# Masked self-attention with a residual: range checks and loads moved behind the first queries, tails last in the last product, eight buffers and later additions for inactive tokens

## The chip, the cores and the metric

The kernel runs on one core of one Trainium2 chip. The metric is the device time of one execution in microseconds (us); lower is better. A core has TensorE (PE; its weight loads are listed as PEld), VectorE (DVE), ScalarE (ACT), GpSimd (POOL) and SyncE (SP). Each engine works through its own queue of instructions in order. SP issues the plain DMAs, POOL the indirect ones that gather and scatter rows by an index.

## The reference

Sixteen batches of x (512 features x 1024 tokens), a mask of zeros and ones by token, and two 512 x 512 weights. Eight heads of 64 features; queries, keys and values are the same projection.

```python
xt = transpose(x, (0, 2, 1))
q = xt @ Wq.T
qh = q.reshape(B, T, NH, dk).transpose(0, 2, 1, 3)
scores = scale * einsum('bhqd,bhkd->bhqk', qh, qh)
logits = (scores * cmask + (1.0 - cmask) * NEG) * rmask
attn = softmax(logits, axis=-1)
ctx = einsum('bhqk,bhkd->bhqd', attn, qh)
out = ctx.transpose(0, 2, 1, 3).reshape(B, T, D) @ Wo.T
return x + transpose(out, (0, 2, 1))
```

About half of the tokens are masked. An active token attends to the active tokens alone. For a masked token all logits are zero, so its attention is the plain mean over all 1024 tokens and its output is the same for all masked tokens of a batch.

## The kernel before

**Compaction.** For each batch the kernel gathers the active tokens into slots 0 to 543 (`C` = 544: four blocks of 128 and a tail of 32, `CT`) and computes attention on these. Inactive tokens sit in further slots, gathered in blocks j = 5 to 8 (the last of 96 rows); they get one row per batch added, the projected mean (`ub`), and are scattered to the output. A flag at the end says whether the inputs were in the ranges on which this rests (`ok`); only if not, a general path runs.

**Work of one batch.** `gather` fetches the slots' rows (`xa`, tail `xt`, L313). `xt` transposes them on TensorE (L398) and `xsplit` splits them into two float16 parts `xh` and `xl` (L358 on ScalarE, L359 on VectorE). `query(n, e, g)` multiplies by the split weights `wqh`, `wql` (L421; feature block e, half g of the columns), ScalarE evicts (L424), VectorE masks the upper columns (L427). `qsplit` splits a query block into float16 parts `hl` (L435 to L437) and SP spreads them over partitions into `xx` by four DMAs (L442 to L445). `value` transposes q (L467), ScalarE copies it to `v` (L469) and squares are summed for each token (L458, L459). `shift`, made of `top` (L505 to L511) and `bottom` (L518 to L532), turns the largest of these sums into a shift `nm` for the exponential. `scores` multiplies `xx` with itself (L580; the tail rows L555) and ScalarE takes the exponential with row sums (L584, L559). `attend` multiplies by `v` (L598, L601). `recip_sums` and `recip_rows` invert the row sums (L620 to L628), transpose them (L634), and send them through DRAM to a broadcast tile `rb` (L639, L642); `norm` multiplies and splits the context (L665 to L671). `project` multiplies with the split `wo` (L681), adds x (L686) and scatters the block (L765). The tails of two or three batches form a group, which is projected in one product, `project_tail`.

**Means.** The mean over all tokens comes from the untransposed x: SP loads it (`load_half` L337, in halves of 256 KB for batches 0 and 1; `load_all` L348, 512 KB a piece, for the others) and ScalarE sums it (`sum_half`, L343).

**Range checks.** `range_x` takes the largest absolute value of each of the four blocks of `xh` (L366, L368); `range_w` takes that of `wqh` and of `woh` in one instruction each (L373); `ranges` compares all of them at the end (L378 to L386).

**Inactive tokens.** `late` gathers a block into the tile `xi`, of which there are four buffers; `rest` adds `ub` on VectorE (L752) and scatters. The first loads of x for batches 0 and 1 use the same tag `xi`.

**What sets the order.** The framework's scheduler orders each engine's instructions from the order of the program, from priorities (`high_priority`) and from dependences; `behind(ins)` lets the instructions inside it be issued after `ins`, and `once(instruction, ins)` adds a dependence that the instruction waits for on the chip. The first queries of batch 0 are written out as the list `first`. From `self.paced = True` on, `run` walks over 18 steps in each batch (`S`: four pairs of heads times four token blocks, and two tail steps): it issues the scores of this step, then a share of the list `m`, in which the rest of this batch and the preparation of the next one stand with their costs, and the transfers that are due. Gathers and scatters are posted to two lines, `urgent` and `spare`, and at each step one of them is issued (`issue`); it waits for `self.beat`, the last score or query product of TensorE at that point. `self.st[0]["top"]` is the instruction that completes the first shift `nm` (L523). The weights `wo` are loaded by `load("o", c)` (L155) and split by `split` (L162 on ScalarE, L163 on VectorE).

**The end.** `last` makes the last batch's output product: the contributions of three pairs of heads first, then `norm` of the fourth pair, then the remaining products. The product of the tails is cut into three pieces that stand between those of the four blocks.

## Time and profile before

| | |
|---|---|
| Time, median of 3 runs (lowest to highest) | 1118.86 us (1118.13 to 1123.56) |
| The profiled execution: its time, its span | 1119.63 us, 1117.8 us |
| PE busy | 1071.0 us (96%) |
| DVE busy | 731.6 us (65%) |
| ACT busy | 676.8 us (61%) |
| POOL busy | 288.6 us (26%) |
| Moved by DMA | 181.34 MB, mean 162 GB/s |

The profile is of one execution; its span runs from the first to the last instruction. A line of the timeline gives start, duration, engine, line of the kernel, operation, out<-in, shape, count and in brackets the engine's idle time before it with what ended it. A line of the waits reads: who waited, for whom, total us, times, longest. A line of windows gives the stretch, its length, each engine's busy time with the number of instructions, the granted TensorE clock, the busy share of the DMA engines and GB/s.

### The profile page before, as it was taken

To read this page: it belongs to the slowest core of one execution; us is meant where nothing else is said; L and a number is where in the kernel's file an instruction comes from. 1 tells how busy PE (TensorE), PEld (TensorE's weight loads), DVE (VectorE), ACT (ScalarE), POOL (GpSimd) and SP (SyncE) were. 2 spreads that over 40 slices of the span, in tenths; PEclk is the share of its full clock that TensorE was granted. 3 is DMA by queue.
4 is the path that set the end of the run, shared out by engine and by line. 5 is a ranking of instruction groups with operands and counts; after the bars stand their busy time and mean duration, and the time that the engine had idled before them with its cause. 6 is when DMAs were issued, how large, how long until landed. Compare 5 with 4: busy or idle time off the path is not lost.

```text
span 1117.8 us, 23184 instructions
## 1 busy us (share of the span) xinstructions
PE 1071.0 (96%) x8386; PEld 697.7 (62%) x8386; DVE 731.6 (65%) x2369; ACT 676.8 (61%) x1716; POOL 288.6 (26%) x303
## 2 busy tenths in 40 slices
PE   7899999999999999999999999999999999998987
PEld 6576666666666666566666666666666666665543
DVE  6787466765665767667665766857576685655543
ACT  5876666666566666567565665666566666645540
POOL 3101031323202222222222232222222223214542
PEclk9999999999999999999999999999999999999999
DMA  7745455646546464565655566465656654546652
GB/s 235 212 121 155 128 164 150 190 127 185 144 128 177 125 209 142 163 179 159 192 145 173 158 185 182 130 193 146 198 157 176 185 146 146 147 115 194 187 168 72
DMA packets 78121, 181.34 MB, mean 162 GB/s; under 512 B 15008, under 2 KB 16800, under 8 KB 78000
## 3 DMA queue, kind: packets, MB, share of 16 engines
q1 hardware_dynamic: 56816, 111.62, 36.4%
q0 software_dynamic: 21184, 68.18, 19.2%
q8 instruction: 68, 1.11, 0.4%
q14 instruction: 53, 0.43, 0.1%
HBM read 92.34 MB, written 33.91 MB: 113 GB/s over the span
## 4 chain that ended last, share of the span: by engine, by line
PE 63%; DVE 14%; DMA 10%; issue 7%; ACT 3%; POOL 2%; SPq 1%; DVEq 0%; POOLq 0%; ACTq 0%
PE pav L598 17%; PE pss L580 16%; PE pm L681 13%; PE pm L421 8%; DMA xi<-x_in,idx 3%; DMA rb<-rd 2%; PE pm L398 2%; PE pav L601 2%; DMA rd<-rr 2%; ACT p L584 2%; POOL y_out L765 2%; PE pm L467 1%; DVE c L665 1%; PE pm L634 1%; DVE tmp L458 1%
## 5 line engine op out<-in xcount | busy, mean ns | idle before, releaser
L584 ACT ACTIVATE p<-pss,nm 128x544 f32<-128x544 f32 x512 | 363.8, 715 | 219.9 <-PE pss L580 209.6
L580 PE MATMUL pss<-xx 128*128 128x272 f16 x2048 | 303.1, 280 | 5.4 <-DMA xx<-hl 2.6
L598 PE MATMUL pav<-p,v 128*64 128x272 f32 x2048 | 278.9, 402 | 0.9 <-ACT c L605 0.9
L580 PEld LDWEIGHTS <-xx 128*128 128x128 f16 x2048 | 192.4, 99 | 85.2 <-issue 40.2
L598 PEld LDWEIGHTS pav<-p,v 128*64 128x64 f32 x2048 | 131.0, 136 | 98.2 <-issue 38.5
L765 POOL DMA_INDIRECT y_out<-xa,idx x68 | 70.9, 1043 | 304.8 <-PE pss L580 163.6
L421 PE MATMUL pm<-xh,wqh 128*128 128x274 f16 (+1 forms) x512 | 143.7, 281 | 0.1
L421 PE MATMUL pm<-xl,wqh 128*128 128x274 f16 (+1 forms) x512 | 143.2, 280 | 0.2 <-DVE xl L359 0.2
L421 PE MATMUL pm<-xh,wql 128*128 128x274 f16 (+1 forms) x512 | 143.2, 280 | 0.0
L313 POOL DMA_INDIRECT xa<-x_in,idx x68 | 69.3, 1020 | 181.7 <-PE pss L580 89.8
L421 PEld LDWEIGHTS <-wqh 128*128 128x128 f16 x1024 | 99.7, 99 | 23.1 <-issue 4.7
L584 ACT ACTIVATION_READ_ACCUMULATOR p<-pss,nm 128x1 f32 x512 | 102.9, 201 | 0.0
L686 DVE SCALAR_TENSOR_TENSOR xa<-pm,xa 128x512 f32<-128x512 f32 x60 | 41.4, 689 | 87.1 <-PE pm L681 87.0
L313 POOL DMA_INDIRECT xi<-x_in,idx x60 | 59.7, 995 | 145.7 <-PE pss L580 49.0
L424 ACT ACTIVATE q<-pm 128x272 f32<-128x272 f32 (+1 forms) x128 | 51.2, 400 | 69.0 <-PE pm L421 68.7
L681 PE MATMUL pm<-woh,ch 128*128 128x512 f16 x240 | 91.1, 380 | 1.0 <-DVE xa L686 1.0
L681 PE MATMUL pm<-woh,cl 128*128 128x512 f16 x240 | 91.0, 379 | 0.0
L681 PE MATMUL pm<-wol,ch 128*128 128x512 f16 x240 | 90.9, 379 | 0.0
L765 POOL DMA_INDIRECT y_out<-xi,idx x60 | 60.3, 1004 | 89.6 <-PE pss L580 70.6
L665 DVE TENSOR_TENSOR c<-c,rb 128x544 f32<-128x544 f32 x64 | 46.3, 724 | 54.7 <-DMA rb<-rd 48.4
L681 PEld LDWEIGHTS <-ch 128*128 128x128 f16 x480 | 46.3, 98 | 41.8 <-issue 1.2
L752 DVE TENSOR_TENSOR xi<-xi,ub 128x512 f32<-128x512 f32 (+1 forms) x60 | 40.1, 687 | 40.6 <-DMA xi<-x_in,idx 27.7
(191 smaller groups left out, 1584.7 us busy)
## 6 DMA issues: line engine op xcount, KB each, us to landing
xx<-hl SPq DMA_DIRECT2D x256, 136.0 KB
xm<-x_nat_in SPq DMA_DIRECT2D x56, 512.0 KB
rb<-rd SPq DMA_DIRECT2D x128, 136.0 KB
pt<-c SPq DMA_DIRECT2D x64, 136.0 KB
pt<-p SPq DMA_DIRECT2D x64, 136.0 KB
ub<-ud SPq DMA_DIRECT2D x16, 256.0 KB
xi<-x_nat_in SPq DMA_DIRECT2D x8, 256.0 KB
xa<-x_in,idx POOLq DMA_INDIRECT x68, 4.3
```

Source lines behind the costliest of these rows:

```text
L313: dma = self.nc.gpsimd.indirect_dma_start(out=tile[:n], out_offset=None, in_=self.x, in_offset=bass.IndirectOffsetOnAxis(ap=idx, axis=0))
L398: self.pe = nc.tensor.transpose(pt[:, c, :], x[:n, c * P:(c + 1) * P], self.ident[:n, :n]).ins
L421: self.beat = nc.tensor.matmul(pq, lhsT=w[:, c, e * P:(e + 1) * P], rhs=xx[:, c, cols], start=(k == 0), stop=(k == 3 * DC - 1)).ins
L424: nc.scalar.activation(s["q"][:, e, cols], pq, AF.Copy, scale=1.0 / (SX * SW))
L580: self.beat = nc.tensor.matmul(pt[:, g, :CH], lhsT=xx[:, 2 * k, i * P:(i + 1) * P], rhs=xx[:, 2 * k + a, g * CH:(g + 1) * CH], start=(a == ...
L584: self.exp = [nc.scalar.activation(t.rearrange("p (g c) -> p g c", g=2), pt[:, :, :CH], AF.Exp, bias=s["nm"][p // HG][:, p % HG:p % HG + 1 ...
L598: nc.tensor.matmul(s["pav"][k * DK:(k + 1) * DK, g, :CH], lhsT=s["v"][p][:, i, k * DK:(k + 1) * DK], rhs=ps[k][:, cols], start=(i == 1), s ...
L665: nc.vector.tensor_tensor(c, c, s["rb"][p], ALU.mult)
L681: nc.tensor.matmul(po[:cols.stop - cols.start], lhsT=a[:, e, cols], rhs=w[:, e, :], start=(e == 0 and k == 0), stop=(e == DC - 1 and k == 2))
L686: self.nc.vector.scalar_tensor_tensor(x, po, 1.0 / (SX * SW), x, ALU.mult, ALU.add)
L752: self.nc.vector.tensor_tensor(x[:n], x[:n], s["ub"][:n], ALU.add)
L765: dma = self.nc.gpsimd.indirect_dma_start(out=self.out, out_offset=bass.IndirectOffsetOnAxis(ap=idx, axis=0), in_=x, in_offset=None)
```

## The change

It does six things.

1. The range checks of batch 0 and of `wq` are placed behind the first shift (`apart`), and `range_w` is done in four pieces, one for each block of 128 rows; `big` and `okr` get a column for each piece.
2. Of the eight halves of batch 1's x, the first four are loaded where all eight were; the other four are posted at the first paced step and wait for the first shift. Their sums are placed at earlier steps (`k // 3` for `k // 2`).
3. The loads of `wo` and batch 2's loads of x wait for the first shift, too.
4. In `last` the product of the tails is made in one piece behind the four blocks.
5. The tag `xi` has eight buffers instead of four, and the additions of `rest` wait for `self.beat`.
6. The memory in SBUF for descriptors of POOL's DMAs is 4096 bytes a partition (`dynamic_dma_scratch_size`) instead of the default 16384.

```diff
-        self.big = fixed("big", [P, self.B + 2])
+        self.big = fixed("big", [P, self.B + 2 * DC])
...
     def load_half(self, b, k, after=None):
         c, h = k // 2, k % 2
-        t = self.sb([P, T // 2], F32, *((("xm", 2), ("ub", 3), ("xi", 4), ("xi", 4))[k // 2 if b < 2 else 0]))
+        t = self.sb([P, T // 2], F32, *((("xm", 2), ("ub", 3), ("xi", 8), ("xi", 8))[k // 2 if b < 2 else 0]))
...
-    def load_all(self, b, c):
+    def load_all(self, b, c, after=None):
         t = self.sb([P, T], F32, "xm", 2)
-        self.nc.sync.dma_start(out=t, in_=self.x_nat[b, c * P:(c + 1) * P, :])
+        self.once(self.nc.sync.dma_start(out=t, in_=self.x_nat[b, c * P:(c + 1) * P, :]), after)
...
-    def range_w(self, name):
-        wh = self.w[name][0]
-        k = self.B + "qo".index(name)
-        self.nc.vector.tensor_reduce(self.big[:, k:k + 1], wh, AX.XY, ALU.max, apply_absolute_value=True)
+    def range_w(self, name, c):
+        k = self.B + DC * "qo".index(name) + c
+        self.nc.vector.tensor_reduce(self.big[:, k:k + 1], self.w[name][0][:, c, :], AX.X, ALU.max, apply_absolute_value=True)
...
-    def late(self, b, j, tag="xi", bufs=4):
+    def late(self, b, j, tag="xi", bufs=8):
...
         def add():
             x, idx = s["xi"][j]
             n = idx.shape[0]
-            self.nc.vector.tensor_tensor(x[:n], x[:n], s["ub"][:n], ALU.add)
+            self.once(self.nc.vector.tensor_tensor(x[:n], x[:n], s["ub"][:n], ALU.add), self.beat)
...
         self.norm(b, 3)
-        tails = slice(0, len(self.group[b]) * CT)
-        self.product(*s["ct"], tails, pos[4], range(1))
         for i in range(4):
-            if i == 2:
-                self.product(*s["ct"], tails, pos[4], range(1, 3))
             self.project(b, i, pos[i], range(3, DC))
-        self.project_tail(b, pos[4], range(3, DC))
+        self.project_tail(b, pos[4])
...
-        first += [(0, lambda k=k: self.load_half(1, k, self.last_xt)) for k in range(2 * DC)]
+        first += [(0, lambda k=k: self.load_half(1, k, self.last_xt)) for k in range(DC)]
...
         with self.behind(self.st[0]["top"]):
             for _, f in query(0, 1, 1)[1:] + query(0, 2, 1)[1:]:
                 f()
+        first_top = self.st[0]["top"]
+        def apart(f, *a):
+            def run():
+                with self.behind(first_top):
+                    f(*a)
+            return run
...
-        begin += [(0, L(self.load, "o", c)) for c in range(DC)]
-        begin += [(0, L(self.range_x, 0, c)) for c in range(DC)] + [(0, L(self.range_w, "q"))]
+        begin += [(0, L(self.load, "o", c, None, first_top)) for c in range(DC)]
+        begin += [(0, apart(self.range_x, 0, c)) for c in range(DC)] + [(0, apart(self.range_w, "q", c)) for c in range(DC)]
...
-                places = [("xi", 4), ("xa", 13)]
+                places = [("xi", 8), ("xa", 13)]
...
             if b == 1:
-                m.append((0, L(self.range_w, "o")))
+                m += [(0, L(self.range_w, "o", c)) for c in range(DC)]
...
-                    free.setdefault(at, []).append(L(self.load_all, b + 2, c))
+                    free.setdefault(at, []).append(L(self.load_all, b + 2, c, None if b else first_top))
...
             if b == 0:
                 for k in range(3, 2 * DC):
-                    free.setdefault(k // 2, []).append(L(self.sum_half, 1, k))
+                    if k >= DC:
+                        free.setdefault(0, []).append(lambda k=k: self.load_half(1, k, first_top))
+                    free.setdefault(k // 3, []).append(L(self.sum_half, 1, k))
...
-    nc = bacc.Bacc("TRN2", target_bir_lowering=False, num_devices=1)
+    nc = bacc.Bacc("TRN2", target_bir_lowering=False, num_devices=1, dynamic_dma_scratch_size=4096)
```

More of the change, by code (lines that the diff above doesn't have):

```diff
@@ L368, in range_x @@
             nc.vector.tensor_reduce(self.big[:, b:b + 1], s["top4"], AX.X, ALU.max)
-    def range_w(self, name):
-        wh = self.w[name][0]
-        k = self.B + "qo".index(name)
-        self.nc.vector.tensor_reduce(self.big[:, k:k + 1], wh, AX.XY, ALU.max, apply_absolute_value=True)
+    def range_w(self, name, c):
+        k = self.B + DC * "qo".index(name) + c
+        self.nc.vector.tensor_reduce(self.big[:, k:k + 1], self.w[name][0][:, c, :], AX.X, ALU.max, apply_absolute_value=True)
     def ranges(self):
         nc, B = self.nc, self.B
-        ok = self.sb([P, B + 2], F16, "okr")
+        ok = self.sb([P, B + 2 * DC], F16, "okr")
         nc.vector.tensor_scalar(ok[:, :B], self.big[:, :B], XMAX, None, ALU.is_le)
         nc.vector.tensor_scalar(ok[:, B:], self.big[:, B:], WMAX, None, ALU.is_le)
-        pe = self.pm([P, B + 2])
+        pe = self.pm([P, B + 2 * DC])
         nc.tensor.matmul(pe, lhsT=self.on16, rhs=ok, start=True, stop=True)
```

## The prediction

> **What bounds the kernel now.** I read the page's busy row first, then who waited for whom, then the timeline where the longest waits lie.

> ```profile
> span 1117.8 us, 23184 instructions
> PE 1071.0 (96%) x8386; PEld 697.7 (62%) x8386; DVE 731.6 (65%) x2369; ACT 676.8 (61%) x1716; POOL 288.6 (26%) x303
> ...
> PE pm L634 <- DVE rcol L628: 6.5, 6, 2.3
> PE pm L467 <- DVE q L427: 6.4, 7, 2.6
> ...
> PE pss L580 <- DMA xx<-hl: 2.6, 2, 2.2
> ...
> DVE xi L752 <- DMA xi<-x_in,idx: 27.7, 21, 3.6
> ```

> TensorE is busy for 96% of the span, so all that can be won is its 46.8 us of idle time (1117.8 − 1071.0). The wait rows give total, times and longest: TensorE waits for VectorE at the row sums (L634) and the query transposes (L467), once for the first split queries (L580). VectorE in turn stands 27.7 us in front of the inactive tokens' additions (L752), whose gather has not landed. By windows of about 65 us the middle is 96 to 99% busy; the idle time lies in 0–55 us and after 1010 us.

> The start, from the timeline and from windows of 4 us (length, busy times, granted clock, DMA share, GB/s):

> ```profile
> 29.70 2.28 DVE L373 TENSOR_REDUCE big<-wqh 128x1 f32<-128x2048 f16 x1
> 33.18 0.62 PE L580 MATMUL pss<-xx 128*128 128x272 f16 x4 [2.25 <-DMA xx<-hl]
> 36.00 0.71 ACT L584 ACTIVATE p<-pss,nm 128x544 f32<-128x544 f32 x1 [3.83 <-DVE nm L520]
> 24.00:28.00 4.00, 2.73 (x20) 1.76 (x18) 4.00 (x9) 2.55 (x6) 1.68 (x2) 1.00 1.01 358
> 28.00:32.00 4.00, 2.93 (x24) 2.21 (x23) 3.89 (x8) 3.60 (x11) 1.24 (x2) 1.00 0.96 238
> 32.00:36.00 4.00, 1.95 (x15) 1.34 (x16) 1.07 (x6) 0.17 (x3) 0.64 (x1) 1.00 0.99 357
> ```

> VectorE (third busy time) is full until 32 us, partly with range checks nobody needs yet, and the DMA engines are full (share about 1) with eight halves of x; the first exponential starts at 36.00.

> Late, and at the end:

> ```profile
> 1017.27 0.69 DVE L752 TENSOR_TENSOR xi<-xi,ub 128x512 f32<-128x512 f32 x1 [2.96 <-DMA xi<-x_in,idx]
> 1020.37 0.33 PE L467 MATMUL pm<-ident,q 128*128 128x128 f32 x1 [2.55 <-DVE q L427]
> 1019.26:1022.67 3.41, 1.52 (x10) 1.00 0.83 228
> 1022.67:1026.08 3.41, 2.89 (x13) 0.50 0.91 267
> 1106.20 0.96 POOL L765 DMA_INDIRECT y_out<-xa,idx  x1 [12.43 <-DVE xa L686]
> 1111.71 0.96 POOL L765 DMA_INDIRECT y_out<-xa,idx  x1 [0.30 <-issue]
> ```

> An addition blocks VectorE for 2.96 us, the mask L427 behind it is late, TensorE stands 2.55 us, and the next 3.41 us are granted half the clock. The kernel ends with five scatters on POOL, 1106.20 to 1111.71.

> **The change, part by part.** The sum is made against the profiled execution, 1119.63 us (span 1117.8), which is 0.77 us above the median of three, 1118.86.

> *Start.* Taken from VectorE ahead of the first scores: L366 at 24.53 (0.63 us up to the next start), two at 26.83 (1.26), L368 and L373 at 29.64–31.90 (2.26); the one at 22.36 stood before an instruction that waited for TensorE anyway and counts nothing. The row maxima L507 then come not at 32.45 but about 29.6; L509, L511, L518, L520 took 1.3 us (34.66 to 35.96) and now run among the query products, so the shifts nm are there at about 31.2. The other half is the xx transfer. Its split L436 is 0.63 us earlier, and 1 MB of x is no longer ahead of it: 1.05 MB at the 358 GB/s of that window is 2.9 us. The first scores could start at 33.18 − 3.5 = 29.7, before the query products end (30.93), so TensorE goes on at 31.2 with the two small products in between. First exponential about 31.7 instead of 36.00: 4.3 us.

> Behind it ScalarE is full (4.00 of 4 us at 36–44 in the same table). The four wo casts there (0.65 + 0.63 + 0.63 + 0.65, L162 from 42.96) move behind the next xm sum, into 56–68 us where ScalarE was busy 3.38, 1.74 and 2.14 of 4: up to 2.2 us more. Against that VectorE gets the range work at about 33–40: 4 x 0.71, and wq in four pieces. A 512-element piece is not in the trace: between 2.28/4 = 0.57 and the 0.71 of the 545-element L366; I take 0.68, nearer in shape, 2.7 in all and 5.6 with L368. Its cover is VectorE's 5.5 us of idle time at 32–44 (1.07, 3.10 and 2.32 busy of 4), of which the shift leaves about half, and four wol splits (0.69 each) that leave this stretch; without cover the second query's split and its scores are 2 us late. The waits added to loads stand in SP's queue: behind two halves of x, which wait for the shifts (first_top), come the spreads of queries 1 and 2; their hl is itself made after first_top, so they lose 2 x 0.5 us of issue and 0.5 MB of bandwidth (1.5 us). The wo loads and batch 2's xm are now behind query 3's spread, some 15 us later than 31.06; readers are the casts at about 56. Taken: −4.5, ends −2 and −6.5.

> *Additions and eight buffers, 55–1010 us.* A new buffer spares POOL's gather its wait for an old scatter (4.7 us in 3 waits) and the tie to a score product (beat) puts L752 later in VectorE's order, some after L427 instead of before it. TensorE waits just behind a waiting addition at 450 (1.5 us), and with 0.2 to 0.4 us at 247, 508, 715 and 906: about 3 us to win. The price: 60 of 64 additions wait for TensorE too, and behind them now stand L620, L626–L628 (for L634) about twice as often, 0.69 us each. No row shows that wait, so bounds: −3 if VectorE is always late anyway, +5 if seven of them come through. Taken −1, near the gain, because an addition behind beat starts when TensorE has just issued scores and has 1 to 2 us of other work.

> *1010–1026.* The gathers at 1013.77 and 1015.68 waited 1.86 and 0.88 us for scatters to free the buffer; with eight they don't. Without the 2.96 us L427 runs at about 1017.0, before TensorE needs it at 1017.8: 2.55 us. The half-clock window did 1.45 us less than its 2.89 busy. [...] I take −4.0; the wait at L634 (1.30) stays, as one more addition stands before L628.

> *1058–1084.* Additions that wait 3.65 and 2.05 us move behind L628 and L686: TensorE's 0.64 and most of 1.01 go, and the rb transfer that VectorE awaits at 1077.88 is about 1.9 us earlier. But two additions (1.3 us) now lie between it and L628 at 1082.38. Net −0.6, ends −2.5 and +1.5.

> *Tail.* Without the first tail piece (0.77 us, 1103.60 to 1104.37) in front of it, block 0 and its scatter are 0.77 earlier, at 1105.43; the other four follow at POOL's step of 1.27: last at 1110.5 for 1111.71. The tails' twelve products (12 x 0.216) end at 1108.9, its addition at 1109.7, in time. −1.2.

> *At nothing.* wo's range in pieces: 0.4 us of VectorE time in a stretch where it has 14 us of slack (50.52 of 65). [...]

> Sum: 4.5 + 1 + 4 + 0.6 + 1.2 = 11.3. 1119.6 − 11.3 = 1108.3, and 1107.6 beside the median.

> **The rivals.** (1) Only start and tail pay, the new waits eating the rest: −5.7, 1113.2. For it: few of the 27.7 us reach TensorE. Against: the chain 1017 to 1020 is plain. (2) The gain at the start is handed back, as ScalarE's sums or VectorE stand for loads that now come later, and the middle gives nothing: −1.2 to −3, about 1117. For it: VectorE and ScalarE are both full at 36–53. Against: the casts that leave. (3) The other side: the additions' new wait becomes the bound. About 30 of them stand right before the row sums; each that comes through is 0.69 us at L634. All 30 are +20.7 − 11.3: 1128. It turns to a loss from 17 on. For it: L634 and L467 are already TensorE's longest waits; against: in 49 of 64 cases L634 did not wait for VectorE. (4) The order does not change as said: excluded for the start, as the order of instructions shows L373 behind the second query's split and the loads behind the spreads.

> **How the numbers follow.** A measurement tells 0.5%, 5.6 us, from no change: faster is below 1113.3. Likeliest case 0.64 (1101 to 1112; by the ends of its terms a little more); rival 1 0.20, two thirds of it just below 1113.3; rival 2 0.08; rival 3 0.08. Faster 0.64 + 0.14, same 0.06 + 0.08, slower 0.08. The range from 1101 to 1117 leaves out some 0.06 below, part of rival 2 and rival 3.

> **What would show it.** Right: the first L584 at 31–33 us; no L580 wait on xx over 1 us before 40; L752 waits on xi under 12 us in total; no half-clock window between 1000 and 1060; last scatter 1.0 to 1.4 us nearer to the first. Wrong: TensorE waits at L634 well over 12.7 us in total (6.5 + 4.9 + 1.3 before), ScalarE waiting for wo, xi gathers spaced wider than 1.3 us.

## The result and the profile after

The changed kernel takes 1102.14 us (median of 4 runs, 1100.26 to 1102.9), the kernel before 1118.49 us beside it (1116.53 to 1123.56). The ratio is 0.9832, 95% interval 0.9808 to 0.9855: 16.4 us less by the medians. The forecast of 1107.6 had the direction, but 11.3 of the 16.4 us; with the ratio on 1118.86 the time is 1100.1, just under the range of 1101 to 1117. The profiled execution has a span of 1100.9 us and a time of 1102.9.

The page's busy row and the waits of the changed kernel (who waited, for whom, total us, times, longest):

```profile
span 1100.9 us, 23215 instructions
PE 1066.3 (97%) x8386; PEld 695.1 (63%) x8386; DVE 735.7 (67%) x2375; ACT 675.8 (61%) x1716; POOL 295.2 (27%) x303
...
PE pss L555 <- DMA xx<-hl: 2.7, 1, 2.7
PE pm L634 <- DVE rcol L628: 2.4, 4, 0.8
...
PE pm L467 <- DVE q L427: 0.7, 2, 0.4
...
DVE xi L752 <- PE pss L580: 17.2, 20, 1.9
DVE xi L752 <- DMA ub<-ud: 11.7, 4, 3.5
```

TensorE's work is nearly the same (1066.3 for 1071.0); its idle time fell from 46.8 to 34.6 us. The waits for the row sums (L628) fell from 6.5 to 2.4 us and for the query mask (L427) from 6.4 to 0.7. VectorE's 27.7 us in front of the additions for a gather are gone. In their place stand 17.2 us for TensorE's scores, which is the tie itself, and they cost TensorE nothing that shows.

**Where the time went.** Both kernels take the same 512 exponentials L584 in the same order of batches, so the two traces can be cut at the 1st, 33rd, 193rd, 225th, 449th, 481st and last. The windows between those, of before and then of the changed kernel (stretch, length, each engine's busy time, granted clock, DMA share, GB/s):

```profile
36.00:97.00 61.00, 57.83 (x484) 39.79 (x482) 46.80 (x165) 46.86 (x123) 6.60 (x6) 1.00 0.59 160
97.00:433.00 336.00, 328.26 (x2574) 214.60 (x2572) 222.11 (x726) 209.21 (x528) 72.95 (x71) 1.00 0.54 155
433.00:502.00 69.00, 66.45 (x529) 43.09 (x528) 47.30 (x163) 42.01 (x106) 17.66 (x18) 1.00 0.56 160
502.00:963.60 461.60, 455.55 (x3583) 298.89 (x3582) 310.35 (x994) 290.74 (x738) 125.12 (x124) 1.00 0.58 167
963.60:1036.30 72.70, 68.48 (x512) 43.93 (x510) 44.91 (x138) 38.22 (x99) 21.74 (x22) 0.98 0.52 145
1036.30:1091.30 55.00, 50.46 (x355) 28.04 (x355) 27.10 (x82) 28.49 (x75) 26.68 (x27) 0.97 0.58 176
```

```profile
33.20:95.00 61.80, 58.64 (x487) 39.97 (x486) 50.80 (x175) 47.00 (x123) 7.15 (x7) 0.97 0.67 195
95.00:428.70 333.70, 328.18 (x2574) 214.71 (x2572) 222.09 (x725) 208.67 (x529) 72.81 (x71) 1.00 0.54 157
428.70:495.00 66.30, 65.30 (x524) 42.34 (x523) 47.58 (x163) 41.48 (x105) 18.08 (x18) 1.00 0.58 167
495.00:957.10 462.10, 455.93 (x3586) 299.22 (x3585) 312.25 (x995) 290.81 (x737) 128.82 (x124) 1.00 0.57 167
957.10:1025.50 68.40, 67.28 (x513) 43.16 (x512) 45.66 (x140) 38.27 (x99) 22.96 (x22) 1.00 0.53 154
1025.50:1074.80 49.30, 48.76 (x355) 27.12 (x354) 27.54 (x78) 28.35 (x75) 28.34 (x27) 1.00 0.61 192
```

Up to the first exponential −2.8; then +0.8, −2.3, about −2.2 (the cut at 502 is half a microsecond late, which the next row takes back), 0, −4.3, −5.7; behind the last one 26.5 became 26.1, −0.4. The sum is −16.9, the difference of the spans. The two late rows carry 10 of it. They have the granted clock of 0.98 and 0.97 in before (a window of 3.41 us at half clock in each) and 1.00 after.

The start of the changed kernel, from the timeline, and two windows of it:

```profile
33.22 0.71 ACT L584 ACTIVATE p<-pss,nm 128x544 f32<-128x544 f32 x1
39.31 0.28 PE L555 MATMUL pss<-xx 128*32 128x272 f16 x1 [2.65 <-DMA xx<-hl]
37.18:40.60 3.42, 1.29 (x11) 1.00 (x12) 2.77 (x6) 2.18 (x6) 0.00 (x0) 1.00 0.96 254
40.60:44.01 3.41, 3.41 (x26) 1.51 (x25) 1.89 (x5) 1.26 (x3) 0.00 (x0) 0.50 0.65 200
```

The first scores no longer wait for xx; the second query's transfer of xx is now the late one, TensorE stands 2.65 us for it, and a window at half clock follows. Late and at the end, in the timeline:

```profile
1012.50 0.68 DVE L752 TENSOR_TENSOR xi<-xi,ub 128x512 f32<-128x512 f32 x1
1016.89 0.32 DVE L427 TENSOR_TENSOR q<-q,hr 128x160 f32<-128x160 f32 x1
1068.36 0.33 PE L634 MATMUL pm<-ident,rcol 128*128 128x128 f32 x1 [0.54 <-DVE rcol L628]
1089.56 0.96 POOL L765 DMA_INDIRECT y_out<-xa,idx  x1 [12.34 <-DVE xa L686]
1094.62 0.90 POOL L765 DMA_INDIRECT y_out<-xg,tails  x1 [0.30 <-issue]
```

The addition at 1012.50 has no bracket: its rows are there. The transpose L634 stands 0.54 us; in before it stood 2.30, in a window in which TensorE was 1.50 us busy, and the next window was at half clock:

```profile
1082.61 0.33 PE L634 MATMUL pm<-ident,rcol 128*128 128x128 f32 x1 [2.30 <-DVE rcol L628]
1080.70:1084.11 3.41, 1.50 (x12) 0.84 (x12) 1.98 (x9) 1.13 (x4) 0.93 (x2) 1.00 0.77 226
1084.11:1087.52 3.41, 3.41 (x17) 2.23 (x14) 0.00 (x0) 1.46 (x5) 0.41 (x1) 0.50 0.53 154
```

### The profile page after: what moved, and what is told of

Same layout as the page of the kernel before. It is cut to its first block, busy times and chain, and to the rows that moved or that the text cites. A ratio compares the mean times of both kernels' runs of the same rounds, so it can differ in the third digit from the quotient of the medians.

```text
span 1100.9 us, 23215 instructions
## 1 busy us (share of the span) xinstructions
PE 1066.3 (97%) x8386; PEld 695.1 (63%) x8386; DVE 735.7 (67%) x2375; ACT 675.8 (61%) x1716; POOL 295.2 (27%) x303
## 4 chain that ended last, share of the span: by engine, by line
PE 72%; DVE 14%; DMA 6%; issue 4%; ACT 3%; SPq 1%; POOL 0%; DVEq 0%; POOLq 0%; ACTq 0%
PE pav L598 20%; PE pss L580 17%; PE pm L681 15%; PE pm L421 8%; PE pm L398 3%; PE pav L601 2%; DMA rb<-rd 2%; PE pm L467 2%; DVE c L665 2%; PE pm L634 1%; DMA rd<-rr 1%; ACT p L584 1%; PE pss L555 1%; DVE top L366 1%; DVE tmp L458 1%
## 5 line engine op out<-in xcount | busy, mean ns | idle before, releaser
L584 ACT ACTIVATE p<-pss,nm 128x544 f32<-128x544 f32 x512 | 363.2, 714 | 215.2 <-PE pss L580 208.0
L580 PE MATMUL pss<-xx 128*128 128x272 f16 x2048 | 301.6, 280 | 0.1
L580 PEld LDWEIGHTS <-xx 128*128 128x128 f16 x2048 | 192.1, 99 | 77.9 <-issue 33.7
L421 PE MATMUL pm<-xh,wqh 128*128 128x274 f16 (+1 forms) x512 | 143.4, 280 | 0.1
L765 POOL DMA_INDIRECT y_out<-xa,idx x68 | 69.4, 1021 | 275.2 <-PE pss L580 169.5
L421 PE MATMUL pm<-xl,wqh 128*128 128x274 f16 (+1 forms) x512 | 142.9, 279 | 0.2 <-DVE xl L359 0.2
L421 PE MATMUL pm<-xh,wql 128*128 128x274 f16 (+1 forms) x512 | 143.1, 279 | 0.0
L313 POOL DMA_INDIRECT xa<-x_in,idx x68 | 68.7, 1010 | 183.8 <-PE pss L580 89.4
L421 PEld LDWEIGHTS <-wqh 128*128 128x128 f16 x1024 | 99.4, 99 | 23.1 <-issue 5.1
L584 ACT ACTIVATION_READ_ACCUMULATOR p<-pss,nm 128x1 f32 x512 | 102.8, 201 | 0.0
L313 POOL DMA_INDIRECT xi<-x_in,idx x60 | 61.8, 1030 | 142.7 <-PE pss L555 50.8
L686 DVE SCALAR_TENSOR_TENSOR xa<-pm,xa 128x512 f32<-128x512 f32 x60 | 41.4, 689 | 80.6 <-PE pm L681 80.4
L765 POOL DMA_INDIRECT y_out<-xi,idx x60 | 67.1, 1119 | 99.1 <-PE pss L580 51.0
L343 ACT ACTIVATE xm<-xm 128x1024 f32<-128x1024 f32 (+1 forms) x60 | 61.9, 1032 | 2.3 <-DMA xm<-x_nat_in 2.3
```

What stands on the lines that cost most here:

```text
L313: dma = self.nc.gpsimd.indirect_dma_start(out=tile[:n], out_offset=None, in_=self.x, in_offset=bass.IndirectOffsetOnAxis(ap=idx, axis=0))
L343: self.nc.scalar.activation(s["xm"][k], s["xm"][k], AF.Copy, accum_out=s["ms2"][:, k:k + 1])
L421: self.beat = nc.tensor.matmul(pq, lhsT=w[:, c, e * P:(e + 1) * P], rhs=xx[:, c, cols], start=(k == 0), stop=(k == 3 * DC - 1)).ins
L580: self.beat = nc.tensor.matmul(pt[:, g, :CH], lhsT=xx[:, 2 * k, i * P:(i + 1) * P], rhs=xx[:, 2 * k + a, g * CH:(g + 1) * CH], start=(a == ...
L584: self.exp = [nc.scalar.activation(t.rearrange("p (g c) -> p g c", g=2), pt[:, :, :CH], AF.Exp, bias=s["nm"][p // HG][:, p % HG:p % HG + 1 ...
L686: self.nc.vector.scalar_tensor_tensor(x, po, 1.0 / (SX * SW), x, ALU.mult, ALU.add)
```

## The experiments

All times are medians beside runs of the kernel before on the same chip. Beside the five groups of runs the kernel before took 1118.5, 1121.2, 1121.6, 1123.6 and 1125.3 us, so ratios are compared, not times across groups; a figure in us that comes from a ratio is that ratio times the kernel before of its group. The kernels named s_ are before plus a part; a_ and c_ are the changed kernel less a part, or with one thing more.

**The parts one by one: start, eight buffers, tie, tails.** The edits are items 1 to 3 of the change (s_start), item 6 with the first half of 5 (s_buf8), the second half of 5 (s_later), and item 4 (s_tails), each put alone into before. For s_later it is one line:

```diff
-            self.nc.vector.tensor_tensor(x[:n], x[:n], s["ub"][:n], ALU.add)
+            self.once(self.nc.vector.tensor_tensor(x[:n], x[:n], s["ub"][:n], ALU.add), self.beat)
```

s_start: 

> Before plus the start alone: range checks in pieces and behind the first shifts, second halves of batch 1's x, batch 2's x and the wo loads behind the first shifts. Forecast's theory (start gains 4.5 and keeps it): 4.5 us less than before. Rival, from matching the same exponentials in the two traces (first one 2.78 us earlier, the gain down to 0.9 at the 15th, 2.2 from the 40th on): about 2 us less. Both: first exponential at 32 to 33.5 us, last pieces of the kernel unchanged, both late half-clock windows (near 1020 and 1082) still there.

s_buf8: 

> Before plus the eight buffers and the smaller descriptor memory alone. Theory 'buffers' (the late additions wait because their gathers wait for old scatters): VectorE's 27.7 us of waits on xi at L752 fall under 10, both late half-clock windows go, 9 to 12 us less than before. Theory 'order' (the wait is only worth what it blocks, and that is decided by where the addition stands): L752 still waits over 15 us, 0 to 4 us less. [...]

s_later: 

> Before plus the additions' tie to the score product alone, with four buffers. Theory 'order': L752 waits on xi fall under 12 us because the additions stand later, both late half-clock windows go, 9 to 12 us less than before. Theory 'buffers': the gathers at 1014 and 1016 still wait for scatters, the additions still block VectorE, 0 to 4 us less. The forecast's third rival (the tie itself costs): up to 5 us more.

s_tails: 

> Before plus the last product's tails put last, alone. Forecast: 1.2 us less, last scatter about 1.2 nearer to the last split L671 than the 8.43 us of before. By the changed kernel's trace (6.59 us there): 1.8 us less. Rival (the tails' addition comes too late for the fifth scatter): no change.

| beside a before of 1121.23 us | us | ratio, 95% interval | less by |
|---|---|---|---|
| s_start | 1113.77 | 0.9936 (0.9918 to 0.9955) | 7.2 |
| s_buf8 | 1114.73 | 0.9946 (0.9921 to 0.9971) | 6.1 |
| s_later | 1110.03 | 0.9895 (0.9873 to 0.9916) | 11.8 |
| s_tails | 1122.15 | 1.0002 (0.9982 to 1.0023) | −0.2 |

The last column is the ratio on 1121.23. s_start gives more than either theory had (its first exponential is at 33.5); why is seen below. The tie (the additions' dependence on `self.beat`) is the largest part, and theory "order" holds for it: of the waits of VectorE, with four buffers and the tie, then with eight buffers and no tie,

```profile
DVE xi L752 <- PE pss L580: 17.0, 19, 1.9
```

```profile
DVE xi L752 <- DMA xi<-x_in,idx: 27.0, 19, 4.3
```

the eight buffers leave the additions waiting as long as before (27.7), and the tie alone removes that wait entirely. In s_later the late transpose L634 stands 0.73 us, as little as in the changed kernel:

```profile
1073.76 0.33 PE L634 MATMUL pm<-ident,rcol 128*128 128x128 f32 x1 [0.73 <-DVE rcol L628]
```

Yet s_buf8 gains 6.1 where "order" allowed 4: its trace loses the stall at 1017 to 1022 (4.7 us between the 449th and the 481st exponential, against before), because the gathers there no longer wait for scatters (three such waits, 4.7 us, in before; none in s_buf8). s_later loses the same stall, with the three waits still there (5.2 us). So the two overlap there, and the four parts sum to 24.9 where the whole gives 18.8 (0.9832 on the same 1121.23).

**The two halves of the start.** s_ranges has item 1 alone, s_loads items 2 and 3 alone.

s_ranges: 

> Before plus the range checks alone (in pieces, those of batch 0 and wq behind the first shifts); the loads stay where they were. If the range checks on VectorE are what delayed the start (forecast: row maxima L507 from 32.45 to about 29.6): the shifts come by 32, but the first scores still wait for the xx transfer behind 1 MB more of x, first exponential 34 to 36 us, 1 to 3 us less than before. If the loads are the whole cause: no change. If the checks are: the same 7 us as the whole start.

s_loads: 

> Before plus the delayed loads alone; the range checks stay ahead of the first shifts. If the loads delayed the start: the wait for xx at L580 near 33 us (1.9 to 2.5 us in the kernels with the old start) shrinks under 1, so the half-clock windows near 35 us go too, 3 to 6 us less than before although the shifts are not earlier. If VectorE's range checks set the first exponential: 0 to 2 us less.

Beside a before of 1121.63: s_ranges 1115.68, ratio 0.9949 (0.993 to 0.9969), s_loads 1116.22, ratio 0.9951 (0.9933 to 0.9968): 5.7 and 5.5 less, each nearly the 7.2 of both. For the loads the first theory (3 to 6) holds; the checks give more than the 1 to 3 expected, with the first exponential at 33.8. Whether the two overlap or add up is not settled: each figure has an interval of about 2 us to both sides. Counted in the traces from the first query product (L421) to the 33rd exponential, s_ranges takes 78.5 us and s_loads 78.7, six profiles with the old start 79.5 to 83.2 (mean 81.7), seven with the new one 75.3 to 77.7 (mean 76.4): 3.2 and 3.0 us of 5.3, which would add up. s_loads shows no half-clock window before 446 us, and its wait at the first L580 is

```profile
31.63 0.64 PE L580 MATMUL pss<-xx 128*128 128x272 f16 x4 [0.17 <-DMA xx<-hl]
```

**Parts taken out of the changed kernel: tie, buffers, descriptor memory, start, tails.**

a_not_later: 

> The changed kernel without the additions' tie to the score product (eight buffers kept). If the tie carries the late gain (alone it gave 11.8 us): 5 to 8 us more than the changed kernel, about 1108 to 1110 beside a before of 1121. If the eight buffers do the same work by themselves: within 2 us of the changed kernel. Sum of the parts run alone without the tie (7.2 + 6.1 + 0 below before): 1108.

a_buf4: 

> The changed kernel with four buffers and the old descriptor memory. If the tie makes the buffers superfluous (alone: tie 11.8, buffers 6.1, together with the start's 7.2 they would be 25, and the changed kernel has 16 to 19): within 2 us of the changed kernel, VectorE's waits on xi at L752 still under 5 us. If both are needed: 4 to 6 us more.

a_buf4_small: 

> The changed kernel with four buffers but the small descriptor memory. If the descriptor memory costs nothing (forecast): the same as with four buffers and the old memory, 4 us above the changed kernel, 1105 to 1107. If the small memory costs up to 3 us that the eight buffers hide: 1107 to 1109. If it is the memory's size and not the buffers that makes the last 4 us: the changed kernel's 1102.

a_old_start: 

> The changed kernel with the old start (range checks and loads as before; tie, eight buffers and tails kept). Forecast's size of the start: 4.5 us more than the changed kernel, 1107. By the start alone on the kernel before (7.2 us): 1109 to 1110. By matching exponentials of the two first traces (2.2 us left at the 40th): 1104 to 1105, if the trace of before was a typical start; it showed no half-clock window in its first 60 us, while three other kernels with the old start show one of 6.8 us near 35 us, so 4 to 6 more is expected here, with a wait of about 2 us for xx at the first L580 and that window again.

c_after (the changed kernel unedited): 

> The changed kernel itself, beside the next three on one chip. By its first ratio, 0.983 of before whatever the chip: 1100 to 1104. If the last four kernels were high because their chip is slow for the changed kernel as well: 1104 to 1107.

c_old_start: 

> The changed kernel with the old start, once more, now beside its control. Forecast's size: 4.5 us above the control. By the start alone on the kernel before: 7.2 above. By the two first traces: 2 above.

c_tails_first: 

> The changed kernel with the last product's tails in their old place (first piece ahead of block 0, the rest after block 1). Forecast: 1.2 us above the control. By the last split L671 to the last scatter in the traces (8.43 us old, 6.59 new): 1.8 above. If tails last gain nothing (alone 0): equal.

| kernel | us, before beside it | ratio, 95% interval |
|---|---|---|
| a_not_later | 1109.14, 1121.63 | 0.9889 (0.9868 to 0.991) |
| a_buf4 | 1106.19, 1121.63 | 0.9871 (0.9849 to 0.9893) |
| a_buf4_small | 1108.24, 1123.59 | 0.9865 (0.9842 to 0.9888) |
| a_old_start | 1113.33, 1123.59 | 0.9915 (0.9899 to 0.9931) |
| c_after | 1108.41, 1125.26 | 0.9839 (0.9817 to 0.9861) |
| c_old_start | 1114.34, 1125.26 | 0.9898 (0.9876 to 0.9919) |
| c_tails_first | 1109.06, 1125.26 | 0.9847 (0.9824 to 0.987) |

c_after, the control, has the first ratio again, on a chip that is 6 to 7 us slower for both kernels; the expected 1100 to 1104 forgot the chip.

*Tie.* Without it the changed kernel gives back 0.0057 of the ratio, 6.4 us. The trace of a_not_later shows the mechanism at 443 us, a place that cost before 1.54 us; the timeline and the windows:

```profile
443.02 0.69 DVE L752 TENSOR_TENSOR xi<-xi,ub 128x512 f32<-128x512 f32 x1 [1.72 <-DMA xi<-x_in,idx]
444.89 0.32 DVE L427 TENSOR_TENSOR q<-q,hr 128x160 f32<-128x160 f32 x1
445.26 0.33 PE L467 MATMUL pm<-ident,q 128*128 128x128 f32 x1 [1.70 <-DVE q L427]
443.49:446.90 3.41, 1.71 (x11) 0.99 (x11) 3.41 (x13) 1.72 (x5) 1.04 (x1) 1.00 0.84 255
446.90:450.30 3.40, 3.40 (x16) 1.77 (x15) 3.40 (x14) 0.48 (x2) 0.00 (x0) 0.50 0.75 171
```

The addition waits for its rows, the mask behind it is late, TensorE stands, and the next window is at half clock: 4.1 us more between the 193rd and the 225th exponential than in the changed kernel.

All 18 profiles together, by what they have of the tie and of the eight buffers (us from one exponential to the other, lowest to highest):

| | tie (11 profiles) | eight buffers, no tie (2) | neither (5) |
|---|---|---|---|
| 193rd to 225th | 66.3 to 67.4 | 70.2, 70.4 | 68.2 to 70.9 |
| 449th to 481st | 68.3 to 69.5, one 74.6 (a_buf4_small) | 67.7, 68.0 | 72.2 to 74.1 |
| 481st to last | 49.3 to 52.6 | 53.1, 55.1 | 53.0 to 55.0 |
| late wait at L634 for VectorE | 0.3 to 1.1 | 2.3, 2.4 | 2.1 to 2.3 |

In the first and the third stretch only the tie helps: by the means of the profiles with it and without it 2.7 and 3.5 us, together 6.3 before rounding, where a_not_later gives back 6.4. In the second the tie or the eight buffers do, 4.6 us with a_buf4_small left out. The three sum to 10.9, near the 11.8 of s_later.

*Buffers.* Four buffers seem to cost about 4 us even with the tie (0.0039 of the ratio, with intervals that overlap), against the expected 2 at most. One cause is seen in a_buf4_small, on POOL, VectorE and TensorE:

```profile
1011.39 1.18 POOL L313 DMA_INDIRECT xi<-x_in,idx  x1 [3.36 <-DMA y_out<-xi,idx]
1016.24 0.69 DVE L752 TENSOR_TENSOR xi<-xi,ub 128x512 f32<-128x512 f32 x1 [1.69 <-issue]
1017.98 0.33 PE L509 MATMUL pm<-ident,smcol 128*128 128x128 f32 x1 [3.04 <-DVE smcol L507]
```

The gather waits 3.36 us until an old scatter has landed, and the late addition now blocks the row maxima L507; two half-clock windows follow (L421 takes 0.43 us there, 0.28 ahead of the wait). (The profile names no releaser for this addition; in a_buf4 it starts 0.1 us after its gather has landed.) In a_buf4's profile it waits 0.35 us and nothing follows, so this happens in some executions only (a_buf4_small ran from 1104.5 to 1113.9). What else the four buffers cost stays open. The descriptor memory, for which the forecast's sum has no term, shows no difference: 0.9865 small, 0.9871 default, both with four buffers.

*Start.* The old start (c_old_start) costs 5.9 us against its control c_after (by the ratios 0.0059, 6.6 us, each ratio with an interval of about 2.4 us to both sides). a_old_start, the same kernel on another chip and without a control beside it, has a ratio 0.0076 above c_after's, 8.5 us. The first scores of c_old_start:

```profile
37.48 1.97 PE L580 MATMUL pss<-xx 128*128 128x272 f16 x8 [3.57 <-DMA xx<-hl]
```

That wait was 2.25 us in the profile that the forecast was made from, and it was the shortest but one: in the five other executions with the old start it was 1.87 (eight buffers), 2.43, 2.53, 3.57 and 3.75 us, each followed by two half-clock windows (in c_old_start 0.50 granted from 36.80 to 43.62 us), and the 33rd exponential came at 99.0 to 103.8 us, not at 97.0. With the new start it comes at 94.3 to 96.9 us in ten executions. Part of this lies ahead of the start's own work: in the two latest of the old starts the first query product (L421) stands at 20.5 and 20.7 us, in the others at 17.3 to 19.0. Counted from that product the gain is the 5.3 us found above. Before's 79.5 us is the shortest of its six, and in the first pair the product itself came 1.0 us later in the changed kernel (18.45 for 17.48), as did the first transpose L398 (15.07 for 14.09).

*Tails.* 0.6 us by the medians, not to be told from zero. The traces show a difference. From the end of the copy L637 to the last scatter it takes 15.48 or 15.49 us in all seven profiles with the old tails, although VectorE waited 4.77 to 5.92 us for the rb transfer in this stretch; with the tails last it takes 14.16 to 15.05 us and follows that transfer. So the gain is 0.4 to 1.3 us; with the old tails it is not the transfer that sets the end.

**The new wait at the start, and the half-clock window behind it.**

The late transfer at L555 is that of the second query (the expectations below call it the third transfer). a_spread_first makes the loads of item 2 and 3 wait for the third query's split, so that both spreads of xx go first:

```diff
...
-                        free.setdefault(0, []).append(lambda k=k: self.load_half(1, k, first_top))
+                        free.setdefault(0, []).append(lambda k=k: self.load_half(1, k, third))
```

(`third` is the last copy to `hl` of the third query; the loads of `wo` and of batch 2 wait for it, too.) a_warm and c_warm put idle products in front of the waiting one:

```diff
                 if i is None:
+                    if b == 0 and p == 0:
+                        t = self.ps_av.tile([P, P], F32, tag="av", name="warm")
+                        with self.behind(self.beat):
+                            for _ in range(20):
+                                last = self.nc.tensor.matmul(t, lhsT=self.on16, rhs=self.on16, start=True, stop=True).ins
...
```

a_spread_first: 

> The changed kernel with all loads that wait for the first shifts now waiting for the third query's split, so that both spreads of xx go ahead of the two x halves. If the 0.5 MB and the 0.87 us of issue ahead make the xx transfer late: the wait of 2.65 us at L555 falls to under 1.2, no half clock near 40, 1.6 to 3.5 us less than the changed kernel. If VectorE's splits set it: the wait stays over 2 us, no change. If the later x halves delay ScalarE's sums and batch 1's means: up to 2 us more.

a_warm: 

> The changed kernel with 20 idle products of 128x128 (results unused, about 1.3 us) put in TensorE's wait for the third xx transfer at 36.6 to 39.3 us. By the busy share (in ten profiles each 3.41 us window with TensorE busy under 1.52 us was followed by one at half clock, none over 1.9): that window is 2.6 busy instead of 1.3, no half clock near 40, the wait itself shorter but its end at the same place, 1 to 1.7 us less than the changed kernel. [...] Rival: the products delay the scores, up to 1 us more.

c_warm: 

> The changed kernel with the 20 idle products in the wait for xx near 37 us, once more, now beside its control. If the half-clock window there costs what its busy share says: 1 to 1.7 us below the control. If the window costs nothing, or the products take as much as they save: equal. [...]

a_spread_first: 1108.1 beside 1123.59, ratio 0.9867 (0.985 to 0.9884), not better. The wait at L555 is gone, and the 7th exponential comes 9.9 us after the first (12.9 and 11.2 in the two profiles of the changed kernel); but the 33rd comes 62.5 after it (61.7 and 60.5). What is late next was not followed up. a_warm: 1106.82, ratio 0.9861 (0.9839 to 0.9884); c_warm: 1111.21 beside 1125.26, ratio 0.9878 (0.9855 to 0.99), 2.8 us above its control. Neither profile has a window at half clock there (1.00 granted from 34 to 46 us in both), but no time is gained. One reason is that the window does not always come: in c_after the wait for xx is as long (2.46 us), but no window at half clock follows. Its windows, and then those of c_tails_first, which has the same start:

```profile
36.48:39.90 3.42, 2.11 (x17) 1.35 (x14) 3.42 (x8) 3.17 (x11) 1.50 (x1) 1.00 0.99 319
39.90:43.31 3.41, 2.27 (x27) 1.60 (x27) 3.09 (x7) 1.19 (x4) 0.00 (x0) 1.00 1.04 256
```

```profile
37.69:41.10 3.41, 1.14 (x9) 0.65 (x8) 3.41 (x8) 2.48 (x8) 0.93 (x1) 1.00 0.90 288
41.10:44.51 3.41, 3.41 (x26) 1.77 (x24) 1.69 (x3) 0.12 (x1) 0.00 (x0) 0.50 0.82 247
```

In c_after the idle time falls into two windows and leaves both over 2 us busy. Of the seven profiles with the whole new start and nothing more at that place, two have no such window, four have one and a_not_later has two in a row. With one window the first to the 7th exponential took 12.6 to 13.0 us, without it 11.2 and 11.8: its price is 1.3 us by the means. By these profiles the products should have gained something in most executions; why they did not stays open. The 2.8 us above the control arise after 960 us in the profile, far from the edit; their cause stays open, and the intervals of the two ratios meet. None of these kernels beats the changed one.

## Why the prediction was wrong in size

The step that failed is that for 1058 to 1084: forecast −0.6, and −5.7 in the first two traces, −3.5 by the means of all. The next largest is the middle, −1 for −2.7.

| term | forecast | first two traces | other runs |
|---|---|---|---|
| start | −4.5 | −2.0 | −7.2 alone, −5.9 by putting the old one back; −5.3 by the traces |
| additions and buffers to 1010 | −1 | −4.5 | −2.7 by the traces, at the 193rd to the 225th exponential |
| 1010 to 1026 | −4.0 | −4.3 | −4.6 by the traces |
| 1058 to 1084 | −0.6 | −5.7 | −3.5 by the traces |
| tail | −1.2 | −0.4 | 0 ± 2.3 by time; −0.4 to −1.3 by the traces |

**1058 to 1084 failed as a step.** Its net of −0.6 is the earlier rb transfer, 1.9 us, less two more additions, 1.3; the 1.65 us of TensorE (0.64 and 1.01) that it says go are not in that sum. The runs showed more. First, the copy L637 ahead of rb comes not 1.9 but 3.5 us earlier against TensorE: counted from the 501st exponential (1069.0 in before, 1056.6 in the changed kernel) it was at +3.1 in before (1072.06) and is at −0.4 (1056.17). L628 is 1.9 us earlier, the two additions and a slower transfer (6.40 for 5.82 us) included, and the wait at L634 fell from 2.30 to 0.54, by 1.76. Second, the half-clock window at 1084.11 was left out, although it stands in the profile of before, behind a window of 1.50 us busy: 3.41 us of work at a granted clock of 0.50, by estimate about 1.7 us. With the 1.65 and one wait of 0.58 us at 1046.61 that is also gone, this gives 1.76 + 1.7 + 1.65 + 0.58 = 5.7 in the first pair. The other profiles bear out the first point: the copy L637 is at −0.5 in all 11 with the tie and at +2.8 to +3.1 in all 7 without it, and s_later has nothing but the tie. The second was partly the luck of before's profile: four of the 7 have a half-clock window there, three have none.

**The middle, −1, took a price that was not there.** It set about 3 us to win (the waits that it lists sum to 2.3; at 906 us TensorE has none) against a cost of the tie that no row showed. VectorE does wait 20 times for TensorE in front of the additions, but the wait of TensorE for row sums fell. Two thirds busy, VectorE seems to have room for it. s_later bounds that price: it gains 11.8 with nothing but the tie, so the third rival is out. Of the 4.5 us in the first pair 2.3 lie between the 33rd and the 193rd exponential, where before's profile took 336.0 us and the six others without the tie 332.4 to 334.3, for 333.7 to 336.0 with it; no gain shows there but in that pair.

**1010 to 1026 was right**, with the 1.45 us of the half-clock window: −4.3 in the first pair for −4.0, where the gap of 2.55 us alone would have given −2.55; the granted clock of that stretch rose from 0.98 to 1.00.

**The start was right in mechanism and nearly in size.** −2.0 in the first traces comes from a before that happened to have no half-clock window in its start, and from a changed kernel whose query products came 1.0 us later; the runs put it at 6 to 7 us by time, the traces at 5.3. The second rival (the gain handed back) has only that pair for it: the first 32 steps took 61.0 us in that profile, 62.2 to 63.0 in the other old starts, 61.8 in the changed kernel. The forecast priced the delay of the second query's spread (2 x 0.5 us of issue, 1.5 us of bandwidth), but not that TensorE would stand for it, which takes 2.65 us at L555 and in five of the seven profiles half clock behind it. The delayed loads are not all of that wait: s_ranges, which leaves the loads in their place, has 2.72 us at L555, and s_loads, which moves nothing but the loads, 0.47.

**Tail: right in mechanism.** Its 1.2 lies in the 0.4 to 1.3 of the traces; in the first pair 1.0 us (15.49 to 14.46) is won there, and 0.4 lost ahead of the copy L637 (5.4 us from the last exponential to its end, 4.9 before) and 0.1 behind the last scatter.

Of the signs named, these came as forecast: L752 has no wait for xi (under 12 us expected), there is no half clock between 1000 and 1060, L634's waits for VectorE are 8.6 us (5.5 + 2.4 + 0.7; 12.7 before), ScalarE does not wait for wo. Wrong were the wait for xx (moved to L555, 2.65 us), the first exponential by 0.2 us, and the scatters: from the first to the last it is 5.06 us for 5.51, 0.45 less for the 1.0 to 1.4 expected, since the first became earlier as well.

## What to carry to other kernels

An instruction that may wait for a transfer should not stand in an in-order queue ahead of one that the busiest engine needs (in before the 2.96 us of L752 became 2.55 us of TensorE); tying it to a later event of that engine cost nothing that shows here, where VectorE was a third idle. Price a stall with what follows it: behind TensorE's waits of 1.70 us (a_not_later), 2.30 and 2.55 (before) and 2.65 (the changed kernel) a window at half clock came, behind the 2.46 of c_after none, and in the three stretches compared below such a window cost 1.3 to 1.9 us more; near 1020 us, where wait and window went, both were won (4.3 us for 2.55 and 1.45). A part that acts through one wait in one profile should be sized from several executions: the wait at the start ranged from 1.87 to 3.75 us with the same order there.
